# Single-row fetches of x on two queues replaced by POOL gathers in a graph layer

## The chip, the cores and the metric

The kernel runs on one core of a Trainium2 chip. The metric is the device time of one execution in microseconds; ten executions of the kernel before have a median of 1937.29 us (1935.77 to 1938.89). A profiled execution gives the trace from which everything below is read. Its time is the span from the first to the last instruction, with a little around it.

The names used for the engines are PE (TensorE), ACT (ScalarE), DVE (VectorE), POOL (GpSimd) and SP (SyncE). ACTq, SPq and POOLq are the instruction queues of these engines: there they issue DMAs, move registers and wait.

## What is computed

One message-passing layer over 12,500 nodes with 64 features and 200,000 edges sorted by target node, then a residual and a layer norm. In all of it `ssp(v)` is `softplus(v) - log 2`:

```
nodes       = x[[src, dst]].reshape(E, 128)                 # two rows of x per edge
gates       = (ssp(edge_attr @ We1 + be1) @ We2 + be2) * soft_cutoff(edge_weight)
h           = ssp(nodes @ Wn1 + bn1) @ Wn2 + bn2
message_sum = zeros.at[dst].add(h * gates)                  # sum of the messages by target node
new         = x + ssp(message_sum @ Ws1 + bs1) @ Ws2 + bs2
out         = layernorm(x + new)
```

The part that the change is about is `x[src]`: for each edge one row of 64 floats (256 bytes) of `x`, in DRAM, at an index known only at run time. The rows `x[dst]` are handled otherwise, since the targets are sorted.

## The kernel before, in words

**Groups and slots.** The edges are cut into NG = 391 groups of 512. A group has K = 4 slots of 128 edges, one edge per partition. A slot needs 128 rows of `x`, one per partition, in a tile of 128 x 128 floats: columns 0 to 63 take the row, columns 64 to 105 a one-hot of the edge's target inside a window of 42 nodes. The last slot of the last group is padding, so 1563 slots have to be filled.

**Two ways to fill a slot.** Most slots are filled by `gather` (L221): for each slot of group `g` one indirect DMA at L231, issued by POOL, reads 128 indices from `src_i` and fetches 128 rows into the tile `xg` of the group. `xg` has 19 buffers (`AHEAD` + `BEHIND`), so that POOL can run some 14 groups ahead. The other 47 slots, chosen by `slots_by_rows` (L105), are filled row by row: SP fills 21 of them (slot 3 of some groups) and ACT 26 (slot 2 of some groups). Each row is one ordinary DMA of 256 bytes, at L257 in `fetch`, whose source address is a register. `read_rows` (L245) loads eight such addresses at a time from the tile `rows_i` into registers. The destination is one of two tiles per queue, `xr`, with semaphores of its own (`landed`); `onehot` copies the slot's one-hot into it (L296), and the transpose of the slot (L304) waits for all of its 128 rows.

**One step.** The main loop (L632) does this for one `i` after another, the order of each engine written out by hand. SP issues the loads for group `i + 5` (`load`: the edge features at L278, and at L286 two windows of 42 rows of a table of target rows) and then seven rows of its fetch. POOL issues `gather(i + 14)`. PE transposes the four slots of group `i + 1` (`transposes`, L307, or L304 for a slot by rows). ACT copies the result to SBUF (`xcopy`, L314) and then issues three rows of its fetch. PE does the bias matmuls (L319, L354), the scatter of an older group's messages (L383: messages times one-hots), the two halves of layer 1 (L324, L330). ACT takes `exps` (L341), three rows, `logs` (L344), three rows: nine rows a step. PE does layer 2 of group `i` (L361, L366), DVE its cut and messages (L375, L379), the running sum by node (L400), `softplus` (L349) and the one-hots of group `i + 3` (L293).

From step 378 (`CLOSE`) on the scatter runs one group behind, not two, and step 378 does two scatters. When the sums of a block of 512 nodes are complete, parts of the node network and the layer norm of that block (`node_block`) are worked off among the following steps; L419 and L450 are its matmuls. The last two groups and the last block come after the loop.

**Before the loop** the table of `x @ Wn1[64:] + bn1` is computed for all nodes and written to DRAM (L591 to L595). While it is made, POOL already gathers the first 14 groups (L515). `rows_i` is loaded there (L509) and scaled to byte offsets (L600).

Of the kernel before, what the change touches and what calls it, by code (L numbers as in the profile page):

```python
# [42 lines left out]
F32 = mybir.dt.float32  # L43
BF16 = mybir.dt.bfloat16
I32 = mybir.dt.int32
U8 = mybir.dt.uint8
AF = mybir.ActivationFunctionType
OP = mybir.AluOpType
# [9 lines left out]
P = 128  # L58
D = 64
# [3 lines left out]
DW = D + W  # L63
PIECES = 3
NB = 512
K = 4
# [6 lines left out]


BLOCK_STEPS = ((2, 3, 4, 4, 6, 7, 8, 9, 10, 14), (2, 3, 3, 4, 5, 6, 7, 8, 9, 10), (1, 2, 1, 2, 3))
ROWS = (7, 9)
READ = 8
ROWS_FROM = -1
READY = (5, 7)
LANDED = 4  # L80
CUTOFF = 5.0
EPS = 1e-5
LN2 = 0.6931471805599453
# [18 lines left out]
    return steps  # L102


def slots_by_rows(NG):  # L105

    slots = []
    for queue in range(2):
        n = 0
        for g in range(READY[queue], NG - 2):  # L110
            if (g - READY[queue] - ROWS_FROM + 1) * ROWS[queue] >= (n + 1) * P:
                slots.append((queue, g, K - 1 - queue))
                n += 1
    return slots


def row_columns(NG):

    queues = [queue for queue, _, _ in slots_by_rows(NG)]
    return [-(-queues.count(queue) // READ) * READ for queue in range(2)]  # L120


@with_exitstack
def gnn_resnorm_kernel(ctx: ExitStack, tc: tile.TileContext, a: dict, out: bass.AP, E: int):
    nc = tc.nc
    x = a["x"]
    N = x.shape[0]
    NG = a["eT"].shape[1]
# [5 lines left out]
    assert NCH * P >= N - 1 + W and NR * P >= NH and 8 * D * N < 2**24  # L134
    REST = LOADS + 2

    rows_base = nc.sbuf_base + -nc.sbuf_base % 32
    nc.alloc_sbuf_tensor("rows", [P, 4 * P], F32)
    const = ctx.enter_context(tc.tile_pool(name="const", bufs=1))
    dram = ctx.enter_context(tc.tile_pool(name="dram", bufs=1, space=DRAM))  # L140
    loads = ctx.enter_context(tc.tile_pool(name="loads", bufs=LOADS + 2))
# [42 lines left out]
    rs3 = const.tile([PIECES, K, D], BF16, name="rs3")  # L184
    wns = const.tile([DW, REST, 2, 2 * D], F32, name="wns")

    xgs, xrs, eTs = {}, {}, {}
    made = {}

    def note(key, ins):  # L190
        made.setdefault(key, []).append(ins)
        return ins

    def behind(ins, *keys):

        for key in keys:
            for other in made.get(key, []):
                tc.add_manual_dep(ins.ins, other.ins.name,
                                  mybir.DependencyInfo(mybir.DependencyClass.Sync, mybir.DependencyReason.DATA),
                                  reason="one place of a step takes its waits")  # L200

    slots = slots_by_rows(NG)
    by_rows = {(g, k): n for n, (_, g, k) in enumerate(slots)}
    columns_of = row_columns(NG)
    rows_i = const.tile([P, sum(columns_of)], I32, name="rows_i")
    queues = (nc.sync, nc.scalar)
    firsts = (0, len([1 for queue, _, _ in slots if queue == 0]), len(slots))
    landed = [[tc.alloc_semaphore(f"rows{queue}_{i}") for i in range(LANDED)] for queue in range(2)]
    x_bytes = x.rearrange("(o n) d -> o (n d)", o=1).bitcast(U8)
    table_bytes = table.rearrange("(o n) d -> o (n d)", o=1).bitcast(U8)  # L210

    def arrived(g, k):
        n = by_rows[g, k]
        queue = slots[n][0]
        n -= firsts[queue]
        return landed[queue][n % LANDED], 16 * P * (n // LANDED + 1)

    def padding(g, k):
        return g * GE + k % 2 * HE + k // 2 * P >= E
# [1 line left out]
    def gather(g):  # L221

        xg = loads.tile([P, K, P], F32, name="xg", bufs=AHEAD + BEHIND)
        xgs[g] = xg
        for k in range(K):
            if (g, k) in by_rows:
                continue
            if padding(g, k):
                nc.vector.memset(xg[:, k, :D], 0.0)
                continue  # L230
            note(("gather", g), nc.gpsimd.indirect_dma_start(  # L231
                out=xg[:, k, :D], out_offset=None, in_=x,
                in_offset=bass.IndirectOffsetOnAxis(ap=src_i[:, g, k : k + 1], axis=0)))

    def rows_left(queue):
        return (firsts[queue + 1] - firsts[queue]) * P - fetched[queue]

    def read_rows(i, queue, count):

        count = min(count, rows_left(queue))  # L240
        while i >= ROWS_FROM and len(row_at[queue]) < count:
            q, p = divmod(fetched[queue] + len(row_at[queue]), READ * P)
            assert p % READ == 0
            at = queue * columns_of[0] + q * READ
            row_at[queue] += nc.values_load_multi_w_load_instructions(  # L245
                rows_i[p // READ : p // READ + 1, at : at + READ], engines=[queues[queue].engine], min_val=0,
                max_val=4 * D * (N - 1), skip_runtime_bounds_check_because="src holds rows of x")[1]

    def fetch(i, queue, count):

        for _ in range(min(count, rows_left(queue)) if i >= ROWS_FROM else 0):
            n, r = divmod(fetched[queue], P)
            n += firsts[queue]
            _, g, k = slots[n]
            if r == 0:
                row_tiles[n, "in"], xrs[g, k] = row_tile(queue, n), row_tile(queue, n)
            ins = queues[queue].dma_start(row_tiles[n, "in"][r : r + 1, :D].bitcast(U8),  # L257
                                          x_bytes[:, bass.ds(row_at[queue].pop(0), 4 * D)])
            tc.no_tile_sem_insts.add(ins.ins.name)
            ins.then_inc(arrived(g, k)[0], 16)  # L260
            if r == 0:
                behind(ins, ("rows read", n - 2))
            fetched[queue] += 1

    row_at, row_tiles, fetched = [[], []], {}, [0, 0]

    def row_tile(queue, n):
        return nc.alloc_sbuf_tensor_at(f"xr{queue}_{n % 2}", [P, P], F32,
                                       offset=rows_base + (2 * queue + n % 2) * 4 * P).ap()

    bases = {}

# [18 lines left out]

    def onehot(g):
        last = nc.vector.tensor_tensor(xgs[g][:, :, D:DW], iota, rel[:, g, :].to_broadcast([P, K, W]), OP.is_equal)  # L293
        for k in range(K):
            if (g, k) in by_rows:
                last = nc.vector.tensor_copy(xrs[g, k][:, D:DW], xgs[g][:, k, D:DW])  # L296
                behind(last, ("rows read", by_rows[g, k] - 2))
        note(("onehot", g), last)

    def transposes(g, *needs):  # L300
        tx = tx_tile()[:DW].rearrange("f (k e) -> f k e", k=K)
        for k in range(K):
            if (g, k) in by_rows:
                ins = nc.tensor.transpose(tx[:, k, :], xrs[g, k][:, :DW], ident)  # L304
                note(("rows read", by_rows[g, k]), ins.wait_op(*arrived(g, k), "sem-ge"))
            else:
                ins = nc.tensor.transpose(tx[:, k, :], xgs[g][:, k, :DW], ident)  # L307
            if k == 0:
                behind(ins, *needs)
        xTs[g] = tx  # L310
# [179 lines left out]
    with tc.manual_schedule():  # L490
# [4 lines left out]
        with tc.tile_pool(name="prep", bufs=1) as prep:  # L495
# [10 lines left out]

            for i in range(3):
                load_x(i)
            nc.sync.dma_start(rows_i, a["rows"])  # L509
            dist = cut.rearrange("p g k -> p (g k)")  # L510
            nc.sync.dma_start(dist, a["dist_l"])
            dst_i = rel.bitcast(I32)
# [73 lines left out]
            for i in range(PARTS):  # L586
# [10 lines left out]
                if i == 1:  # L597
                    nc.vector.tensor_copy(base_i[:1], base_b[:1])
                    nc.vector.tensor_scalar(base_i[32:33], base_b[32:33], float(8 * D), None, OP.mult)
                    nc.vector.tensor_scalar(rows_i, rows_i, float(4 * D), None, OP.mult)  # L600
                    for k in range(2):
                        nc.vector.tensor_copy(be3[:, k, :], rows[:, 0, :])
                    for k in range(K):
                        nc.vector.tensor_copy(row3[:, :, k, :], rows[:, 1:3, :])
                        nc.vector.tensor_copy(rs3[:, k, :], rows[:, 3, :])
# [9 lines left out]
        with tc.tile_pool(name="finish", bufs=1) as finish:  # L615
# [16 lines left out]
            for i in range(-1, last - 1):  # L632
                now = parts.pop(i, [])
                early = [part for part in now if part.tensor]
                at(load, i + LOADS)
                read_rows(i, 0, ROWS[0])
                fetch(i, 0, ROWS[0])
                if i >= 0:
                    at(gather, i + AHEAD)
                transposes(i + 1, ("load", i + 1), ("gather", i + 1), ("onehot", i + 1))  # L640
                xcopy(i + 1)
                read_rows(i, 1, ROWS[1])
                fetch(i, 1, ROWS[1] - 6)
                layer1_bias(i + 1)
                at(layer2_bias, i)
                for n, g in enumerate(behind_by(i)):
# [1 line left out]
                layer1_edge(i + 1)  # L648
                layer1_node(i + 1)
                exps(i + 1)  # L650
                fetch(i, 1, 3)
                logs(i + 1)
                fetch(i, 1, 3)
                for g in behind_by(i):
                    window(g)
                at(layer2, i)
# [143 lines left out]
def layouts(inputs):  # L800
# [12 lines left out]
    def padded(v, n, fill):  # L813
        return np.concatenate([v, np.full((n - v.shape[0],) + v.shape[1:], fill, v.dtype)])
# [4 lines left out]

    out = {"x": np.ascontiguousarray(x)}  # L820
    out["src_l"] = lanes(src, 0)
    rows = []
    for queue, columns in enumerate(row_columns(NG)):
        chosen = [out["src_l"].reshape(P, NG, K)[:, g, k] for q, g, k in slots_by_rows(NG) if q == queue]
        v = padded(np.concatenate(chosen), P * columns, 0).reshape(-1, P, READ)
        rows.append(v.transpose(1, 0, 2).reshape(P, columns))
    out["rows"] = np.ascontiguousarray(np.concatenate(rows, axis=1))
    out["dst_l"] = lanes(dst, dst[-1])
    out["dist_l"] = lanes(dist, 1e6)
    out["dst_h"] = np.ascontiguousarray(padded(dst, NR * P * HE, dst[-1]).reshape(NR, P, HE).transpose(1, 0, 2))  # L830
# [42 lines left out]
```

## Time and profile before

| | |
|---|---|
| median of ten runs | 1937.29 us |
| the profiled execution, its time | 1937.95 us |
| the profiled execution, its span | 1936.2 us |
| mean granted clock of PE | 0.972 |
| first row fetch on ACT's queue, on SP's queue (start) | 77.9 us, 81.0 us |
| last row fetch on ACT's queue, on SP's queue (start) | 1813.4 us, 1871.7 us |
| first and last gather on POOL (start) | 3.3 us, 1905.5 us |
| DMA packets, data moved | 150911, 143.53 MB |

How to read it. A group of instructions is given by its line, engine and operation, then `out<-in` by the names of the tiles, the count, the busy time in all and the mean of one in ns, and behind the bar the idle time of the engine just before these instructions with what ended most of it. "issue" is idle time in which the engine waited for nothing that the profile shows. A row of waits is: engine, what it was about to do, what it waited for, us in total, number of times, the longest. A timeline row is: start, duration, engine, line, operation, tiles, shapes, count, and in brackets the idle time before it. Issuing a DMA, moving a register or waiting is not counted as busy, except the gathers on POOL, which POOL works on itself. The spans on POOL are rough.

### The profile page before, as it was taken

Reading aid. Unit: us, or ns where it says so; the run is one execution under the profiler, and the core shown is the slowest. Engines: PE = TensorE matmul, PEld = TensorE weight load, DVE = VectorE, ACT = ScalarE, POOL = GpSimd, SP = SyncE. Lnnn points to the kernel's source line nnn. Section 1 sums busy time; section 2 is a strip of 40 time slices with the busy share of each in tenths; the row PEclk is TensorE's granted clock in tenths of the full one; section 3 lists DMA queues with packets and bytes.
Section 4 is the critical chain, followed back from the end, with each engine's and each line's share of the span. In section 5 each row is a group of like instructions: output and inputs, shape, how many; then the busy total and the mean of one; then the engine's idle time right before and its main releaser. Section 6 shows DMA issues by size and latency. Waiting matters only on the chain.

```text
span 1936.2 us, 47845 instructions
## 1 busy us (share of the span) xinstructions
PE 1789.9 (92%) x11373; PEld 1467.1 (76%) x11373; DVE 1052.9 (54%) x2767; ACT 964.0 (50%) x1318; POOL 1441.0 (74%) x1520
## 2 busy tenths in 40 slices
PE   4899999999999998999999999999999999999997
PEld 4787777877887777777777777777777777777775
DVE  4355555555465554555555555555555555555555
ACT  1255554545455554545555555454454554555543
POOL 7777777777777777777777777777777777777772
PEclk9999999999899999999999999999999999999998
DMA  8422222322222323332322322233223333323321
GB/s 247 132 66 69 65 65 66 71 66 65 68 70 69 68 66 70 71 70 66 71 67 68 76 67 71 68 70 75 68 70 70 71 70 70 73 68 76 74 67 24
DMA packets 150911, 143.53 MB, mean 74 GB/s; under 512 B 51887, under 2 KB 98395, under 8 KB 150626
## 3 DMA queue, kind: packets, MB, share of 16 engines
q1 hardware_dynamic: 94090, 88.26, 16.0%
q0 software_dynamic: 48512, 49.77, 14.1%
q10 hardware_dynamic: 8024, 2.37, 0.6%
q8 instruction: 97, 1.59, 0.3%
q14 instruction: 188, 1.54, 0.3%
HBM read 130.59 MB, written 9.63 MB: 72 GB/s over the span
## 4 chain that ended last, share of the span: by engine, by line
PE 54%; ACTq 13%; issue 8%; SPq 7%; DMA 7%; ACT 6%; DVE 3%; POOL 1%; DVEq 0%; POOLq 0%
PE z L330 12%; ACTq L257 11%; PE gh L366 9%; PE z L383 8%; PE tx L307 6%; PE z L324 6%; PE gh L361 5%; SPq L257 3%; DMA xg<-in_x,src_i 3%; PE gh L354 3%; ACT xT L314 3%; PE z L319 3%; DMA wns<-table 2%; ACTq L245 2%; ACT u L341 2%
## 5 line engine op out<-in xcount | busy, mean ns | idle before, releaser
L231 POOL DMA_INDIRECT xg<-in_x,src_i x1516 | 1440.7, 950 | 465.3 <-issue 358.3
L341 ACT ACTIVATE u<-z 128x768 f32<-128x768 f32 x392 | 317.3, 809 | 698.2 <-PE z L330 660.5
L400 DVE TENSOR_TENSOR sums<-sums,z 64x42 f32 x778 | 152.9, 197 | 771.9 <-ACT u L341 735.2
L330 PE MATMUL z<-xT,wns 106*128 106x256 f32 x1564 | 433.7, 402 | 8.7 <-ACT xT L314 7.9
L344 ACT ACTIVATE u<-u,one 128x768 f32<-128x768 f32 x392 | 366.1, 934 | 70.1 <-ACT u L341 65.5
L366 PE MATMUL gh<-consts,s 128*128 128x64 f32 x3128 | 398.0, 271 | 0.0
L366 PEld LDWEIGHTS gh<-consts,s 128*128 128x128 f32 x3128 | 387.7, 195 | 0.1
L349 DVE SCALAR_TENSOR_TENSOR s<-u,z 128x768 f32<-128x768 f32 x392 | 369.6, 943 | 12.3 <-ACT u L344 10.2
L330 PEld LDWEIGHTS z<-xT,wns 106*128 106x128 f32 x1564 | 303.1, 199 | 81.2 <-ACT xT L314 36.1
L307 PE MATMUL tx<-consts,xg 128*106 128x128 f32 x1517 | 236.7, 276 | 87.8 <-DMA wns<-table 25.5
L383 PEld LDWEIGHTS z<-xg,msg 128*128 128x128 f32 x1556 | 206.2, 193 | 125.5 <-issue 121.2
L314 ACT COPY xT<-tx 106x512 f32<-106x512 f32 x391 | 228.1, 583 | 126.5 <-PE tx L307 106.0
L383 PE MATMUL z<-xg,msg 128*128 128x84 f32 x1556 | 266.8, 294 | 0.9 <-DVE msg L379 0.2
L361 PEld LDWEIGHTS gh<-consts,s 128*128 128x128 f32 x1564 | 247.5, 199 | 25.5 <-DVE s L349 2.0
L324 PE MATMUL z<-eT,consts 128*128 128x256 f32 x782 | 258.4, 413 | 0.0
L307 PEld LDWEIGHTS tx<-consts,xg 128*106 128x106 f32 x1517 | 168.8, 140 | 105.2 <-PE gh L366 52.9
L361 PE MATMUL gh<-consts,s 128*128 128x128 f32 x1564 | 246.9, 281 | 1.7 <-DVE s L349 1.7
L375 DVE TENSOR_TENSOR h<-gh,cut 128x256 f32<-128x256 f32 x391 | 166.1, 425 | 32.8 <-PE gh L366 18.7
L379 DVE TENSOR_TENSOR msg<-gh,h 128x256 f32<-128x256 f32 x391 | 165.9, 424 | 13.4
L354 PE MATMUL gh<-row,ones 3*128 3x512 bf16 x391 | 147.4, 377 | 0.0
L293 DVE TENSOR_TENSOR xg<-consts,rel 128x168 f32<-128x168 f32 x391 | 128.6, 329 | 0.0
L324 PEld LDWEIGHTS z<-eT,consts 128*128 128x128 f32 x782 | 122.7, 198 | 1.5 <-issue 1.5
(93 smaller groups left out, 586.7 us busy)
## 6 DMA issues: line engine op xcount, KB each, us to landing
xr<-in_x ACTq DMA_DIRECT2D x3328, 0.2 KB
eT<-in_eT SPq DMA_DIRECT2D x195, 256.0 KB
xr<-in_x SPq DMA_DIRECT2D x2688, 0.2 KB
xg<-in_x,src_i POOLq DMA_INDIRECT x1516
wns<-table SPq DMA_DIRECT2D x782, 21.0 KB
table<-tb SPq DMA_DIRECT2D x14, 448.0 KB
sums<-in_xT SPq DMA_DIRECT2D x7, 455.0 KB
y<-in_x SPq DMA_DIRECT2D x24, 128.0 KB
```

The costliest lines, as they stand in the source:

```text
L231: note(("gather", g), nc.gpsimd.indirect_dma_start(out=xg[:, k, :D], out_offset=None, in_=x, in_offset=bass.IndirectOffsetOnAxis(ap=src_i[ ...
L257: ins = queues[queue].dma_start(row_tiles[n, "in"][r : r + 1, :D].bitcast(U8), x_bytes[:, bass.ds(row_at[queue].pop(0), 4 * D)])
L307: ins = nc.tensor.transpose(tx[:, k, :], xgs[g][:, k, :DW], ident)
L314: note(("xcopy", g), nc.scalar.copy(xT, xTs[g]))
L324: nc.tensor.matmul(zs[g][:, 0, :HE], we1.rearrange("a h d -> a (h d)"), eTs[g], start=False, stop=True, skip_group_check=True)
L330: nc.tensor.matmul(zn, wns[:, g % REST, h, :], xTs[g][:, h], start=True, stop=True, skip_group_check=True)
L341: nc.scalar.activation(us[g][:, part], z_of(g)[:, part], AF.Exp)
L344: nc.scalar.activation(us[g][:, part], us[g][:, part], AF.Ln, bias=one)
L349: nc.vector.scalar_tensor_tensor(ss[g].rearrange("p i t e -> p (i t e)")[:, part], us[g][:, part], BIG, z_of(g)[:, part], OP.min, OP.max)
L361: nc.tensor.matmul(v[:, 0, t], ss[g][:, 0, t, :], we2, start=False, stop=False, skip_group_check=True)
L366: nc.tensor.matmul(ghs[g][:, 1, 2 * t + h, :], ss[g][:, 1 + h, t, :], wn2, start=False, stop=h == 1 and t == 1, skip_group_check=True)
L383: ins = nc.tensor.matmul(sc, msgs[g][:, 2 * t : 2 * t + 2, :].rearrange("p h f -> p (h f)"), xgs[g][:, 2 * t : 2 * t + 2, D:DW], start=t = ...
```

## The change

All 1563 slots are filled by POOL's gathers. `fetch`, `read_rows`, the list of slots, the tiles `xr` and `rows_i`, their semaphores, the copy of the one-hot into `xr` and the second form of the transpose are removed. Nothing else moves: the order of the loop, the tiles, the number of buffers and the preparation stay.

```diff
-ROWS = (7, 9)
-READ = 8
-ROWS_FROM = -1
-READY = (5, 7)
-LANDED = 4
...
-def slots_by_rows(NG):
...
-def row_columns(NG):
...
-    rows_base = nc.sbuf_base + -nc.sbuf_base % 32
-    nc.alloc_sbuf_tensor("rows", [P, 4 * P], F32)
...
         for k in range(K):
-            if (g, k) in by_rows:
-                continue
             if padding(g, k):
                 nc.vector.memset(xg[:, k, :D], 0.0)
                 continue
             note(("gather", g), nc.gpsimd.indirect_dma_start(
                 out=xg[:, k, :D], out_offset=None, in_=x,
                 in_offset=bass.IndirectOffsetOnAxis(ap=src_i[:, g, k : k + 1], axis=0)))
-
-    def rows_left(queue):
...
-    def read_rows(i, queue, count):
...
-    def fetch(i, queue, count):
...
     def onehot(g):
         last = nc.vector.tensor_tensor(xgs[g][:, :, D:DW], iota, rel[:, g, :].to_broadcast([P, K, W]), OP.is_equal)
-        for k in range(K):
-            if (g, k) in by_rows:
-                last = nc.vector.tensor_copy(xrs[g, k][:, D:DW], xgs[g][:, k, D:DW])
-                behind(last, ("rows read", by_rows[g, k] - 2))
         note(("onehot", g), last)
...
         for k in range(K):
-            if (g, k) in by_rows:
-                ins = nc.tensor.transpose(tx[:, k, :], xrs[g, k][:, :DW], ident)
-                note(("rows read", by_rows[g, k]), ins.wait_op(*arrived(g, k), "sem-ge"))
-            else:
-                ins = nc.tensor.transpose(tx[:, k, :], xgs[g][:, k, :DW], ident)
+            ins = nc.tensor.transpose(tx[:, k, :], xgs[g][:, k, :DW], ident)
...
-            nc.sync.dma_start(rows_i, a["rows"])
...
-                    nc.vector.tensor_scalar(rows_i, rows_i, float(4 * D), None, OP.mult)
...
                 at(load, i + LOADS)
-                read_rows(i, 0, ROWS[0])
-                fetch(i, 0, ROWS[0])
                 if i >= 0:
                     at(gather, i + AHEAD)
                 transposes(i + 1, ("load", i + 1), ("gather", i + 1), ("onehot", i + 1))
                 xcopy(i + 1)
-                read_rows(i, 1, ROWS[1])
-                fetch(i, 1, ROWS[1] - 6)
                 layer1_bias(i + 1)
...
                 exps(i + 1)
-                fetch(i, 1, 3)
                 logs(i + 1)
-                fetch(i, 1, 3)
```

More of the change, by code (lines that the diff above doesn't have):

```diff
@@ L102, in block_steps @@
     return steps
-def slots_by_rows(NG):
[L107 to L114, printed above, removed]
-def row_columns(NG):
-    queues = [queue for queue, _, _ in slots_by_rows(NG)]
-    return [-(-queues.count(queue) // READ) * READ for queue in range(2)]
 @with_exitstack
@@ L185, in gnn_resnorm_kernel @@
     wns = const.tile([DW, REST, 2, 2 * D], F32, name="wns")
-    xgs, xrs, eTs = {}, {}, {}
+    xgs, eTs = {}, {}
     made = {}
@@ L200, in behind @@
                                   reason="one place of a step takes its waits")
[L202 to L209, printed above, removed]
-    table_bytes = table.rearrange("(o n) d -> o (n d)", o=1).bitcast(U8)
[L212 to L216, printed above, removed]
+    table_bytes = table.rearrange("(o n) d -> o (n d)", o=1).bitcast(U8)
     def padding(g, k):
@@ L233, in gather @@
                 in_offset=bass.IndirectOffsetOnAxis(ap=src_i[:, g, k : k + 1], axis=0)))
-    def rows_left(queue):
-        return (firsts[queue + 1] - firsts[queue]) * P - fetched[queue]
-    def read_rows(i, queue, count):
[L240 to L247, printed above, removed]
-    def fetch(i, queue, count):
[L251 to L269, printed above, removed]
     bases = {}
@@ L821, in layouts @@
     out["src_l"] = lanes(src, 0)
[L822 to L827, printed above, removed]
     out["dst_l"] = lanes(dst, dst[-1])
```

## The prediction, written before the changed kernel ran

> **What bounds the kernel now.** I read the page's busy shares first. TensorE, at 92%, looks like the bound, and POOL, at 74%, like an engine with a quarter of the span to spare. Shares cannot settle it, so the next views are POOL's own waits, with its idle time by what ended it, the number of times and the longest, and the page's row of the gathers:
>
> ```profile
> PE 1789.9 (92%) x11373; PEld 1467.1 (76%) x11373; DVE 1052.9 (54%) x2767; ACT 964.0 (50%) x1318; POOL 1441.0 (74%) x1520
> ...
> POOL 7777777777777777777777777777777777777772
> ...
> L231 POOL DMA_INDIRECT xg<-in_x,src_i x1516 | 1440.7, 950 | 465.3 <-issue 358.3
> ```
>
> ```profile
> POOL xg L231 <- issue: 358.3, 1174, 0.3
> POOL xg L231 <- DMA xg<-in_x,src_i: 27.8, 91, 0.3
> POOL xg L231 <- PE z L330: 17.4, 57, 0.3
> ```
>
> The last column is what matters: no idle stretch of POOL before a gather is longer than 0.3 us, whoever is named as its end, except 2.9 us for the first index load. The other engines named in that view only happened to finish then. The timeline of POOL shows the rhythm: start, duration, and the same 0.30 to 0.31 us before every gather.
>
> ```profile
> 14.40 0.95 POOL L231 DMA_INDIRECT xg<-in_x,src_i  x1 [0.31 <-issue]
> 15.65 0.94 POOL L231 DMA_INDIRECT xg<-in_x,src_i  x1 [0.30 <-issue]
> ...
> 1903.04 0.94 POOL L231 DMA_INDIRECT xg<-in_x,src_i  x1 [0.30 <-issue]
> 1904.29 0.95 POOL L231 DMA_INDIRECT xg<-in_x,src_i  x1 [0.30 <-issue]
> 1905.55 0.94 POOL L231 DMA_INDIRECT xg<-in_x,src_i  x1 [0.30 <-issue]
> ```
>
> So POOL issues gathers from 3.35 to 1905.55 us without a pause; one takes 1.25 us from start to start. The "74%" is a saturated queue. Whether TensorE waits for it is read by counting: I laid the start of each group's last gather (in program order, row slots left out) beside the same group's L319, which follows its transposes at once. TensorE is behind that gather by 69 us at group 0 (7.2 against 76.3), 35 at group 100 (497.8, 533.1), 9 at group 200 (983.5, 992.8) and 3.7 at group 230 (1129.0, 1132.7). From there to group 378 the distance stays at 3.2 to 6.6 us, mostly 3.2 to 4: landing and transposes, no store left. At group 380 it is 8.7, at group 390 it is 6.1. So the lead that POOL builds while the table is made is used up by 1130 us, and then POOL sets the pace. TensorE's own step is shorter. These are starts of one step's transposes after the other's, near the end:
>
> ```profile
> 1883.62 0.60 PE L307 MATMUL tx<-consts,xg 128*106 128x128 f32 x4
> ...
> 1887.90 0.60 PE L307 MATMUL tx<-consts,xg 128*106 128x128 f32 x4
> ...
> 1892.17 0.60 PE L307 MATMUL tx<-consts,xg 128*106 128x128 f32 x4
> ...
> 1911.14 0.60 PE L307 MATMUL tx<-consts,xg 128*106 128x128 f32 x4
> ```
>
> A step without a node part takes 4.27 us (1887.90 to 1892.17); one with such a part is longer, and groups 380 to 390 average 4.5. Four gathers take POOL 4 x 1.253 = 5.01 us. The last line is group 390; from its 1911.14 to the end of the span are 25.1 us.
>
> **What the change adds.** 2688 + 3328 rows are 6016, and 6016 / 128 = 47 slots. All 47 become gathers at L231: 1516 + 47 = 1563. The durations are on the page: 0.94 us busy and 0.30 us of issue. The mean pitch from gather 56 (77.29 us) to the last (1905.55) is 1828.26 / 1459 = 1.253 us, stalls included. 47 x 1.253 = **+58.9 us** on the last gather. Bounds: 1.24, the shortest distances, give 58.3; 1.2556, the mean over all 1516 with the stalls of the first 75 us, gives 59.0. No wait is added, and what is queued behind each new gather on POOL is the next gather.
>
> The Trainium skill, DMA: Bandwidth & Descriptors, section "Issuing engines are not separate DMA queues", speaks against this: all issuers end on the same DMA engines, and several issuers only save sequencer time, which is usually small beside the transfer. By that rule moving the slots would cost about nothing and the sum would stay near 0. Here the issuer's 1.25 us is the thing that runs out, while the page's DMA row stands at two to three tenths.
>
> **What it removes, and what hides that.** ScalarE's queue loses 3328 row DMAs at 0.223 us with their moves of 0.029, and 416 register loads of median 0.742, some 1150 us of issue; SP loses 2688 at 0.257 and 336 at 0.804, some 960 us:
>
> ```profile
> L257 ACTq MOVE xr<-in_x x3328: 29/29/41, 77.9 to 1813.4; - x196
> L257 ACTq DMA_DIRECT2D xr<-in_x x3328: 222/223/593, 78.0 to 1813.5; - x196
> ```
>
> These issues hold `xcopy`, `exps` and `logs` behind them, and the chain of waits gives ScalarE's queue 13% and SP's 7% of the span. I take nothing for their removal: it quickens TensorE's step, and that hides under POOL's 5.01 us. The cover is 5.01 - 4.27 = 0.74 us a plain step; if POOL did not pace, all the issue time on the chain could come back at most, 20% of 1936 = 387 us, and at least nothing. The window loads (L286) that were late behind SP's fetches, 25.5 us of TensorE's wait, go the same way: next late is `xg`. VectorE loses 47 copies (L296) of 0.186 us, 8.7 us on an engine 54% busy: nothing. The load and scaling of `rows_i` in the preparation lie before TensorE's first step, with 69 us of lead behind it: nothing. The 47 transposes only change their source (273 ns against 276).
>
> The Trainium skill, SBUF — State Buffer, section "Who interferes with whom", would credit the removed copies to POOL: VectorE and GpSimd share a port pair that a copy in a two-port mode can hold. By that rule up to 8.7 us could come back. The trace barely agrees: of the 54 gathers after 100 us that took over 0.97 us, 4 overlap one of the 44 copies that the timeline lists singly.
>
> The 54 long gathers together exceed the norm by 5.9 us. If their cause were the fetches in any way, the gain would be 5.9 at most; if unrelated, 0. I take 0, since long ones are rare before 600 us too, where fetches run.
>
> **The end.** Behind the last gather come its landing and 25.1 us of last steps and last node block, untouched. What can shrink is TensorE's distance: 6.1 us at group 390 against 3.3 for a group that is taken when it lands. It jumps at group 379 to 380, where two scatters fall in one step and matmuls run at half pace for a step (L330 1.91 us, not 1.03), and then shrinks. From group 380 to 390 TensorE took 45.2 us for its steps and POOL 47.7; with the one row slot of this stretch (at 1898) back on POOL, POOL takes 49.0. With the same jump of 8.7 the distance at the end is 8.7 + 45.2 - 49.0 = 4.9, which is 1.2 less than now. Ends: 3.3 (2.8 less) and 8.7 (2.6 more).
>
> **Sum.** +58.9 - 1.2 = +57.7; I take 57.5. Span 1936.2 + 57.5 = 1993.7. That execution took 1937.95, 1.75 around its span; the median of the runs is 1937.29, 0.7 below it. So 1937.3 + 57.5 = **1994.8 us**.
>
> **Rivals.**
> A, faster: the 0.30 us between gathers is itself caused by the thousands of other DMAs, so POOL quickens when they go, and the freed queues pay. For: 20% of the chain is those two queues. Against: the gathers from 4.7 to 75 us, before the first row fetch at 77.9, show the same 0.30. It decides once the mean pitch is below (1905.55 - 3.35) / 1562 = 1.218 us. At POOL's 0.95 alone TensorE would run free at about 4.5 us: 76.3 + 390 x 4.5 + 24.5 = 1856.
> B, no change: the 14 groups of lead swallow the 47 gathers. For: 69 us of lead exceed 58.9. Against: the lead is spent by group 230. Price 0: 1937.
> C, much slower: a starved TensorE runs its steps at half pace. Such a step (1326.06 to 1331.83) takes 5.77 us, more than 5.01. If every step behind the catching-up were so, from about group 130 (52 us of distance at group 20, shrinking by 0.36 to 0.71 a group): 260 x 0.76 = 198 more, 2192. Against: a slow step leaves TensorE late, the next finds its data there and runs in 4.1 to 4.3; the present distances stay at 3.2 to 6.6.
>
> **How the numbers follow.** The forecast holds 0.92, A 0.015, B 0.015, C or another larger loss 0.05. Range: least 1937.3 + 58.3 - 2.8 - 2.8 (half of the long gathers' 5.9, rounded) = 1990; most 1937.3 + 59.0 + 2.6 = 1998.9, so 1999. About 0.2% (4 us) is what a measurement here can tell from no change. Faster 0.015, the same 0.015, slower 0.97.
>
> **What would show it.** POOL with 1563 gathers at the same 0.94 and 0.30, the last starting near 1964.5; distance near 3.3 us already from some group between 95 and 165, that is from 480 to 830 us; TensorE waiting for `xg` for more than 100 us in all where it now waits 18.0; ScalarE and SP queues without L257 and L245, and off the chain. Wrong if the pitch leaves 1.24 to 1.26, if POOL shows waits over 0.3 us, or if the tail behind the last transposes leaves 24 to 27 us.

## The result and the profile after

The changed kernel takes 1994.58 us, the median of 8 runs (1992.98 to 1996.48), against 1937.29 before: a ratio of 1.0294, 95% interval 1.0285 to 1.0303. It is 57.3 us slower. The profiled execution has a span of 1994.0 us. One thing has to be known for what follows: the experiments ran on three chips, of which one ran the kernel before in 1936.23 us and two in 2672.56 and 2638.19 us, at granted clocks of 0.81 to 0.84, so each run is told by its ratio to the kernel before on its own chip.

The page of the kernel after, busy shares, POOL's and DMA's row of slices, the chain and two groups (the line numbers have moved: L190 is the gather, L222 the transpose, L234 the first matmul behind it):

```profile
PE 1789.4 (90%) x11373; PEld 1480.7 (74%) x11373; DVE 1040.7 (52%) x2719; ACT 953.6 (48%) x1318; POOL 1487.3 (75%) x1567
...
POOL 7777777777777777777777777777777777777773
...
DMA  8422222222222232223222222222222232222221
...
PE 78%; DMA 9%; DVE 4%; issue 4%; POOL 2%; SPq 1%; ACT 1%; DVEq 0%; POOLq 0%; ACTq 0%
...
L190 POOL DMA_INDIRECT xg<-in_x,src_i x1563 | 1487.1, 951 | 479.6 <-issue 341.7
...
L222 PE MATMUL tx<-consts,xg 128*106 128x128 f32 x1564 | 240.6, 277 | 159.4 <-DVE msg L294 62.4
```

The shares have hardly moved: POOL from 74 to 75%, TensorE from 92 to 90%. Nothing in that first line says that 57 us were lost, or where. The gathers' row does: 1563 instead of 1516, 951 ns each instead of 950. The chain shows the two queues gone (ScalarE's 13% and SP's 7% are 0 and 1%), and the kernel is slower all the same.

POOL's waits and its timeline in the kernel after:

```profile
POOL xg L190 <- issue: 341.7, 1121, 0.3
POOL xg L190 <- DMA xg<-in_x,src_i: 58.4, 190, 0.6
POOL xg L190 <- PE z L245: 40.0, 131, 0.3
```

```profile
1963.70 0.94 POOL L190 DMA_INDIRECT xg<-in_x,src_i  x1 [0.30 <-PE z L245]
1964.94 0.94 POOL L190 DMA_INDIRECT xg<-in_x,src_i  x1 [0.30 <-issue]
1966.19 0.94 POOL L190 DMA_INDIRECT xg<-in_x,src_i  x1 [0.30 <-issue]
```

It is the same rhythm with 6016 other DMAs gone: 0.94 and 0.30. Leaving out the first index load (2.9 us), two waits alone are longer than that, 0.57 and 0.53 us, both while the table is still being made:

```profile
17.81 0.94 POOL L190 DMA_INDIRECT xg<-in_x,src_i  x1 [0.57 <-DMA xg<-in_x,src_i]
19.27 0.99 POOL L190 DMA_INDIRECT xg<-in_x,src_i  x1 [0.53 <-DMA xg<-in_x,src_i]
```

The last gather of group 70 with that group's transposes, and the transposes of the last group, on TensorE:

```profile
363.98 0.94 POOL L190 DMA_INDIRECT xg<-in_x,src_i  x1 [0.30 <-DVE msg L294]
...
367.00 0.62 PE L222 MATMUL tx<-consts,xg 128*106 128x128 f32 x4
...
1969.42 0.60 PE L222 MATMUL tx<-consts,xg 128*106 128x128 f32 x4
```

The span can be added up from three places: the start of the last gather, the distance from there to the first matmul behind the last transposes (L319, now L234), and the rest. The kernels before and after, and two experiments that are told below:

| us | before | after | no row fetches, 47 slots unfilled | SyncE's rows only |
|---|---|---|---|---|
| gathers on POOL | 1516 | 1563 | 1516 | 1542 |
| mean pitch from gather 56 on | 1.2531 | 1.2538 | 1.2538 | 1.2537 |
| start of the last gather | 1905.55 | 1966.19 | 1907.36 | 1939.18 |
| distance at group 390 | 6.1 | 3.8 | 5.2 | 4.8 |
| rest to the end of the span | 24.5 | 24.1 | 24.2 | 24.6 |
| span | 1936.2 | 1994.0 | 1936.7 | 1968.6 |
| TensorE's step, groups 10 to 50 | 4.34 | 4.09 | 4.09 | 4.38 |

From before to after the last gather moves by 60.6: 47 x 1.2538 = 58.9 for the gathers, 0.75 because gather 56 already starts later (78.04 against 77.29), and 1.0 because the pitch is 0.7 ns longer over 1459 gathers. The distance gives back 2.4, the rest 0.4. 60.6 - 2.4 - 0.4 = 57.8, the difference of the spans (1994.0 - 1936.2).

### The profile page after: what moved, and what is told of

Read it like the earlier page. It is cut to its first block, busy times and chain, and to the rows that moved or that the text cites. A ratio compares the mean times of both kernels' runs of the same rounds, so it can differ in the third digit from the quotient of the medians.

```text
span 1994.0 us, 35107 instructions
## 1 busy us (share of the span) xinstructions
PE 1789.4 (90%) x11373; PEld 1480.7 (74%) x11373; DVE 1040.7 (52%) x2719; ACT 953.6 (48%) x1318; POOL 1487.3 (75%) x1567
## 4 chain that ended last, share of the span: by engine, by line
PE 78%; DMA 9%; DVE 4%; issue 4%; POOL 2%; SPq 1%; ACT 1%; DVEq 0%; POOLq 0%; ACTq 0%
PE z L245 16%; PE gh L281 13%; PE z L298 11%; PE tx L222 10%; PE z L239 9%; PE gh L276 7%; DMA xg<-in_x,src_i 5%; PE gh L269 4%; PE z L234 4%; DVE h L290 2%; DMA wns<-table 2%; POOL xg L190 2%; PE z L505 2%; DVE msg L294 1%; PE tx L334 1%
## 5 line engine op out<-in xcount | busy, mean ns | idle before, releaser
L190 POOL DMA_INDIRECT xg<-in_x,src_i x1563 | 1487.1, 951 | 479.6 <-issue 341.7
L245 PE MATMUL z<-xT,wns 106*128 106x256 f32 x1564 | 427.2, 397 | 0.6 <-ACT xT L229 0.6
L281 PE MATMUL gh<-consts,s 128*128 128x64 f32 x3128 | 397.7, 271 | 0.0
L281 PEld LDWEIGHTS gh<-consts,s 128*128 128x128 f32 x3128 | 387.7, 195 | 0.1
L222 PE MATMUL tx<-consts,xg 128*106 128x128 f32 x1564 | 240.6, 277 | 159.4 <-DVE msg L294 62.4
L245 PEld LDWEIGHTS z<-xT,wns 106*128 106x128 f32 x1564 | 311.3, 199 | 50.5 <-ACT xT L229 3.4
L222 PEld LDWEIGHTS tx<-consts,xg 128*106 128x106 f32 x1564 | 167.8, 136 | 187.6 <-issue 82.6
```

Source lines behind the costliest of these rows:

```text
L190: note(("gather", g), nc.gpsimd.indirect_dma_start(out=xg[:, k, :D], out_offset=None, in_=x, in_offset=bass.IndirectOffsetOnAxis(ap=src_i[ ...
L245: nc.tensor.matmul(zn, wns[:, g % REST, h, :], xTs[g][:, h], start=True, stop=True, skip_group_check=True)
L281: nc.tensor.matmul(ghs[g][:, 1, 2 * t + h, :], ss[g][:, 1 + h, t, :], wn2, start=False, stop=h == 1 and t == 1, skip_group_check=True)
```

## The experiments

The theory is that POOL's queue sets the end at 1.2538 us a gather once its lead is spent, and that the row fetches neither cost nor gained anything at the end. Its rival is that the freed queues matter on their own, so that the 57 us are a larger loss less a gain. Four runs were made on the chip where the kernel before is at 1936.23 us, and the main readings are from these; eight were made on the other two chips.

**Neither fetched nor gathered.** Against the kernel after, `skip` holding the 47 slots that rows had filled before:

```diff
         for k in range(K):
+            if (g, k) in skip:
+                continue
             if padding(g, k):
```

> The same 47 slots are filled by nobody: neither row fetches nor gathers; the slots keep the rows of an older group. POOL issues 1516 gathers as in the kernel before, SyncE and ScalarE fetch nothing. Theory (POOL's queue sets the end at 1.2537 us a gather, the row fetches cost nothing at the end): 1994.6 - 47 x 1.2537 = 1935.7 us, 1934 to 1938, the time of the kernel before. Rival (the freed queues pay on their own, and POOL's loss was larger than the difference that was measured): below 1925 us.

Measured: 1937.84 us (1937.11 to 1938.51), ratio to the kernel before 1.0006, interval 0.9996 to 1.0015. The rival needed less than 1925. So with the same number of gathers as before, and without a single one of the 6016 row DMAs, their 752 register loads and 47 copies, the time is that of the kernel before. The span and the gathers' row on the page of this run, then its last gather and the transposes of the last group:

```profile
span 1936.7 us, 34994 instructions
...
L206 POOL DMA_INDIRECT xg<-in_x,src_i x1516 | 1443.2, 952 | 464.6 <-issue 327.3
```

```profile
1907.36 0.94 POOL L206 DMA_INDIRECT xg<-in_x,src_i  x1 [0.30 <-issue]
...
1907.95 0.60 PE L238 MATMUL tx<-consts,xg 128*106 128x128 f32 x4
```

12,851 instructions fewer than the 47,845 of before, and 0.5 us of span. This separates the two halves of the change: the removal is worth nothing at the end that this measurement can tell (0.15% at most, some 3 us), and the 47 gathers are the loss.

**SyncE's rows alone.** Against the kernel before:

```diff
-    for queue in range(2):
+    for queue in (0,):
         n = 0
...
```

> SyncE fetches its 21 slots by rows again, ScalarE none; POOL gathers 1542 slots. Theory: 1994.6 - 21 x 1.2537 = 1968.3 us, last gather near 1939.9 us. Rival (ScalarE's freed queue gave part of the loss back): below 1960 us. It also tells which queue had lengthened TensorE's step in groups 10 to 50 (4.34 us before, 4.09 after): ScalarE's if it stays near 4.09 here, SyncE's if it is near 4.34.

Measured: 1971.43 us (1970.44 to 1972.52), ratio 1.0178, interval 1.0161 to 1.0195. The last gather starts at 1939.18 us, where 1939.9 was expected; the time is 3.1 above the forecast and 11 above what the rival needed. Against the kernel after the last gather starts 27.0 us earlier, and the distance and the last steps are 1.6 longer, which makes the spans differ by 25.4; the medians differ by 23.2, where 26.3 were forecast. ScalarE's queue held 13% of the old chain, and taking all its fetches away brought no time beyond what the gathers explain.

```profile
1939.18 0.94 POOL L231 DMA_INDIRECT xg<-in_x,src_i  x1 [0.30 <-issue]
```

The run also shows that SyncE's fetches are enough to lengthen TensorE's step while POOL still has its lead: with SyncE fetching alone the step is 4.38 us, without any fetch 4.09. The same stretch of time in three kernels, in the table of windows (length, then busy us and instruction counts of TensorE's matmuls, its weight loads, VectorE, ScalarE and POOL, the clock, DMA); first before, then SyncE alone, then after:

```profile
125.00:280.00 155.00, 150.99 (x1011) 121.49 (x1010) 85.55 (x220) 83.98 (x108) 117.17 (x124) 1.00 0.29 67
```

```profile
125.00:280.00 155.00, 149.22 (x993) 124.88 (x993) 82.96 (x214) 81.31 (x107) 117.29 (x124) 0.98 0.28 66
```

```profile
125.00:280.00 155.00, 155.00 (x1063) 130.16 (x1062) 88.85 (x229) 86.33 (x114) 117.47 (x124) 1.00 0.30 71
```

Without fetches TensorE does not stop once in 155 us and gets 5% more matmuls done (1063 against 1011). POOL's column is the same in all three, 124 gathers. That is the gain of the change in one row; it comes to nothing at the end, since TensorE only reaches POOL sooner.

**POOL relieved.** Against the kernel after:

```diff
         for k in range(K):
+            if k == 3 and AHEAD + BEHIND <= g < NG - 2:
+                continue
             if padding(g, k):
```

> Slot 3 of groups 19 to 388 is filled by nobody: POOL issues 1193 gathers instead of 1563, the last near 1498 us if it never waits. Theory (TensorE's own step is 4.1 to 4.5 us with the node parts, 5.01 only because of POOL): 79 + 390 x 4.35 + 25 = 1800 us, 1742 to 1860. Rival (TensorE's step is near 4.85 to 5 us for reasons of its own and POOL's pace is a coincidence): 1936 us or more.

Measured: 1759.22 us (2 runs, 1758.04 and 1760.4), ratio 0.9081, interval 0.9063 to 0.9099. That is inside the theory's range and far below the rival's 1936. The page and POOL's waits:

```profile
PE 1706.9 (97%) x11373; PEld 1427.0 (81%) x11373; DVE 1040.0 (59%) x2719; ACT 940.9 (54%) x1318; POOL 1175.4 (67%) x1197
...
PE 96%; DMA 2%; DVE 1%; ACT 1%; issue 0%; SPq 0%; DVEq 0%; ACTq 0%
```

```profile
POOL xg L192 <- PE z L300: 154.8, 287, 1.7
```

This is how POOL looks when it is not the bound: it waits up to 1.7 us for the scatter matmul (L300 here) that frees a buffer, 287 times, its mean pitch is 1.395 us, and the distance of TensorE behind it stays at 60 to 70 us from group 50 on instead of falling to 3.5. The expected start of the last gather, 1498 us, was wrong for the reason that its own sentence left open: POOL did wait, and the last one started at 1662.86. TensorE's step is 4.16 us over groups 50 to 150. As an estimate, 1994.58 - 1759.22 = 235 us is what POOL's pace costs the kernel after.

**The gathers doubled.** Against the kernel after, each of the 47 slots is gathered twice into the same place:

```diff
-            note(("gather", g), nc.gpsimd.indirect_dma_start(
...
+            for _ in range(2 if (g, k) in twice_of else 1):
+                note(("gather", g), nc.gpsimd.indirect_dma_start(
...
```

> The 47 slots that the change moved to POOL are gathered twice, each time into the same place: 1610 gathers, nothing else changed against the kernel after. Theory: 1994.6 + 47 x 1.2537 = 2053.5 us. Rival (part of the 57 us came with the removal of the row fetches, not with the gathers): clearly less than 59 us more, for instance 20 to 40.

Measured: 2133.18 us (2 runs), 138.6 more than the kernel after, where 58.9 were expected. Both theory and rival miss. POOL's waits and one pair of twins in its timeline:

```profile
POOL xg L205 <- DMA xg<-in_x,src_i: 119.7, 218, 2.9
```

```profile
124.38 0.94 POOL L205 DMA_INDIRECT xg<-in_x,src_i  x1 [0.30 <-issue]
127.04 0.94 POOL L205 DMA_INDIRECT xg<-in_x,src_i  x1 [1.72 <-DVE xg L231]
```

The second gather writes where the first writes, and waits until the first has landed: by the trace's records of landings, each second one starts 0.26 us (six times 0.76) after its twin's last landing. The start of this one is 2.66 us after its twin's; the 47 such pitches run from 2.65 to 3.79 and exceed 1.25 us by 81.7 together. 58.9 + 81.7 = 140.6, about the 138.6 found. So the edit added a wait that was not meant, and the run says nothing against the price of a gather. What it gives is the time from a gather's start to its landing, 2.4 us at least. That is most of the floor under the distance: in the kernel after the median landing is 2.5 us, a transpose that waited for it starts 0.35 to 0.46 later, and the transposes take some 0.55, together 3.4 to 3.5 (the distance there is 3.4 at least).

The same with the extra gathers going to spare tiles that nobody reads was run on the chip at 2638.19 us:

```diff
+            if (g, k) in twice_of:
+                nc.gpsimd.indirect_dma_start(
+                    out=loads.tile([P, D], F32, name="spare", bufs=4), out_offset=None, in_=x,
...
```

> As the kernel after, with 47 extra gathers of the slots that the change moved, this time into spare tiles that nobody reads, so that no extra gather waits for the landing of its twin. 1610 gathers. Theory (each gather costs POOL's pitch of 1.2538 us and nothing else): 1994.6 + 58.9 = 2053.5 us. Rival (a gather's price grows with their number, through transfers or landings): near the 2133 us of the run with the twins in one place, or anything over 2065.

Measured: 2704.98 us against 2638.19 for the kernel before there, ratio 1.0257, interval 1.0157 to 1.0358. Both expected times were meant for a chip at 1937; this decides nothing between them.

**The other runs on those chips.** On the chip at 2672.56 us three of the edits above were run (SyncE's rows alone, 47 slots unfilled, 370 slots unfilled) and ScalarE's rows alone (`for queue in (1,):`), which was also run on the chip at 2638.19.

> SyncE fetches its 21 slots by rows again, ScalarE none; POOL gathers 1542 slots. Theory (POOL's queue sets the end at 1.2537 us a gather, and the row fetches themselves cost or gain nothing at the end): 1994.6 - 21 x 1.2537 = 1968.3 us, last gather near 1966.2 - 26.3 = 1939.9 us. Rival (freeing ScalarE's queue, 13% of the old chain, gave part of the loss back, so POOL's price per slot is above 1.25 and ScalarE's fetches cost time of their own): below 1960 us, with less than its share left for the run with ScalarE alone. It also tells which of the two queues had lengthened TensorE's step in groups 10 to 50 (4.34 us before, 4.09 after): ScalarE's if it stays near 4.09 here.

> ScalarE fetches its 26 slots by rows again, SyncE none; POOL gathers 1537 slots. Theory: 1994.6 - 26 x 1.2537 = 1962.0 us, last gather near 1933.6 us. Rival (ScalarE's fetches cost time of their own): above 1970 us. TensorE's step in groups 10 to 50 near 4.34 us if ScalarE's issues are what lengthened it, near 4.09 if SyncE's.

> The same 47 slots are filled by nobody: neither row fetches nor gathers, the slots keep the rows of an older group. POOL issues 1516 gathers as in the kernel before, SyncE and ScalarE fetch nothing. Theory: 1994.6 - 47 x 1.2537 = 1935.7 us, 1934 to 1938, the time of the kernel before, since the row fetches cost nothing at the end. Rival (the freed queues pay on their own and the loss of POOL was larger than the difference): below 1925 us.

> Slot 3 of groups 19 to 388 is filled by nobody (it keeps an older group's rows): POOL issues 1193 gathers instead of 1563, the last near 3.4 + 1192 x 1.2537 = 1498 us if it never waits, and TensorE is released from it. Theory (TensorE's own step is 4.1 to 4.5 us with the node parts, 5.01 only because of POOL): 79 + 390 x 4.35 + 25 = 1800 us, 1742 to 1860. Rival (TensorE's step is near 4.85 to 5 us for reasons of its own and POOL's pace is a coincidence): 1936 us or more.

> ScalarE fetches its 26 slots by rows again, SyncE none; POOL gathers 1537 slots. Theory: 1994.6 - 26 x 1.2538 = 1962.0 us, last gather near 1934 us, and TensorE's step in groups 10 to 50 stays at 4.09 us, since with SyncE alone fetching it was 4.38. Rival (ScalarE's issues, 13% of the old chain, cost time of their own): above 1970 us and a step over 4.2.

| run | us | before there | ratio, 95% interval |
|---|---|---|---|
| SyncE's rows alone | 2620.12 | 2672.56 | 0.975 (0.967 to 0.983) |
| ScalarE's rows alone | 2633.14 | 2672.56 | 0.983 (0.975 to 0.990) |
| 47 slots unfilled | 2625.32 | 2672.56 | 0.981 (0.975 to 0.987) |
| 370 slots unfilled (one run) | 2135.7 | 2672.56 | |
| ScalarE's rows alone, other chip | 2583.47 | 2638.19 | 0.980 (0.970 to 0.989) |

None of the expected times can be compared with these. What the table shows is that the theory has a condition. Here 26 or 21 gathers more than before went with a time 2% shorter, not 1 to 2% longer. The waits of three engines in the run with 47 slots unfilled:

```profile
POOL xg L206 <- PE z L314: 353.0, 113, 62.5
DVE h L306 <- remote: 234.9, 79, 5.9
ACT xT L245 <- remote: 198.4, 78, 5.6
POOL xg L206 <- remote: 167.8, 80, 2.7
```

POOL waits for the scatter that frees its buffers, once for 62.5 us and otherwise up to 6 us at a time, and TensorE stays 87 to 105 us behind it (groups 230 to 378), not 3 to 7: POOL is not the bound there. The same kernel between 1000 and 1500 us, on the chip at 1936.23 us and on this one:

```profile
1000.00:1500.00 500.00, 459.52 (x2964) 378.43 (x2962) 271.22 (x716) 250.28 (x351) 378.42 (x400) 0.98 0.28 67
```

```profile
1000.00:1500.00 500.00, 410.28 (x2249) 332.44 (x2248) 201.99 (x530) 190.17 (x260) 293.56 (x310) 0.82 0.22 51
```

TensorE does 2964 matmuls in this stretch on the one chip and 2249 on the other. On the second, ScalarE and VectorE also stand still together, 74 times and for up to 5.9 us, until a release that the view calls "remote": it can put it to nothing in the profile of this core. At one such stall, which ended at 1205.6 us, TensorE had been idle since 1200.5. What holds them was not found. One run with 370 slots unfilled took 2135.7 us there, 490 less than with 47 unfilled, though POOL was not the bound in it either (TensorE is 68 to 85 us behind); why is open as well. The kernel after itself was not run there, so whether the change costs anything on such a chip is open.

**More rows instead of fewer.** If each row slot saves 1.25 us, more of them should beat the kernel before.

```diff
-ROWS = (7, 9)
+ROWS = (9, 9)
```

The second run has `(9, 12)`.

> The other way: the kernel before with nine rows a step on SyncE instead of seven, so 27 + 26 = 53 slots by rows and 1510 gathers. Theory (POOL still sets the end): 6 x 1.2538 = 7.5 us less than before, 1929.8 us. Rival (SyncE's queue is full at nine rows, its window loads come late and TensorE's step exceeds POOL's): no gain or slower than before.

> Nine rows a step on SyncE and twelve on ScalarE: 27 + 35 = 62 slots by rows, 1501 gathers. Theory: 15 x 1.2538 = 18.8 us less than before, 1918.5 us, as long as the queues hold out: ScalarE's would issue 12 x 0.252 + 1.5 x 0.742 = 4.1 us a step, POOL's pace is (1563 - 62) / 391 x 1.2538 = 4.81 us a step. Rival (the queues become the bound): above 1930 us, with POOL waiting for buffers.

Measured on the chip at 2638.19 us: 2753.98 and 2755.83, ratios 1.046 (1.038 to 1.054) and 1.043 (1.035 to 1.051). On that chip more rows are a loss of 4%. On a chip at 1937 us they were not run, so that more rows than in the kernel before would pay is not shown.

## Why the prediction was right, and where its steps were not

**POOL is saturated at 74%.** Right, and shown twice: with 1516 gathers and no fetches the time is the old one, and with 1193 gathers POOL waits and TensorE sets the end.

**+58.9 for the gathers.** Right in size: 47 x 1.2538. The last gather moved by 60.6, 1.7 more than the term and 1.6 above its upper bound of 59.0: 0.75 were lost in the first 78 us and 1.0 in a pitch 0.7 ns longer. What causes these two was not found.

**Nothing for the long gathers.** Right. Counted alike in both traces (over 0.97 us, after 100 us), there are 55 before and 55 after, 6.0 and 7.7 us above the usual 0.944 (the prediction counted 54 and 5.9): they did not go with the fetches, so the half of 5.9 us that the lower end of the range allows for was not there to be had.

**Nothing for the freed queues.** Right at the end (ratio 1.0006 without them), and right that the gain hides under POOL's 5.01 us. Before that end it is larger than was reckoned with. The step "shrinking by 0.36 to 0.71 a group" put the point where TensorE has used up the lead at group 95 to 165; it came at group 70, near 367 us. The step had taken TensorE's pace from groups in which SyncE was fetching, 4.3 to 4.65 us. Without fetches it is 4.09, so the distance shrinks by 0.92 a group.

**The distance at the end.** Right in sign, small by half: 2.4 less, not 1.2. The assumed term was "the same jump of 8.7". After the step with two scatters the distance in the kernel after is 5.6 at group 380, and 3.8 at group 390.

**Twenty-five microseconds of last steps.** 25.0 before and 24.6 after, from the start of the last transposes to the end, where no change was forecast; the layer 2 matmuls of the last group (L366, now L281) took 1.97 us for eight before and 1.35 after.

The forecast stands on one product. The single terms miss by 1.7, 1.2 and 0.4 us; that they cancel to 0.2 us in the time (1994.58 against 1994.8) is luck.

**What would show it.** The pitch (1.2538), the last gather (1966.19 against 1964.5), the last steps and the idle queues are as said. "Wrong if POOL shows waits over 0.3 us" did occur, with the waits of 0.57 and 0.53 us at 17.8 and 19.3 us; they cost 0.5 us beyond the usual gap, and there is none later, so the sign was set too tight and the mechanism stands. The distance fell at group 70 and not between 95 and 165, as told above. The last sign, "TensorE waiting for `xg` for more than 100 us", seems to fail in the view of TensorE's waits after:

```profile
PE tx L222 <- DVE msg L294: 62.4, 58, 1.3
PE tx L222 <- DMA wns<-table: 24.3, 20, 6.5
PE tx L222 <- DVE h L290: 24.1, 39, 1.0
PE tx L222 <- DMA xg<-in_x,src_i: 18.3, 15, 1.7
```

The row named `xg` is 18.3, about as before. All idle time ahead of the transposes grew from 87.8 (L307) to 159.4 us, and more than half of it is put down to VectorE's messages and cuts, on which by the order of the program no transpose depends. The trace also records when each gather lands, and that settles it: among the 345 groups of the kernel after whose last gather has a full record, 175 have transposes that waited over 0.1 us, and 171 of these, 130 us in all, start 0.2 to 0.5 us behind the last landing of the group's last gather. In the kernel before it is 55 of 92 among 318 groups, and 34 us. So the sign came true, and the view's row hid it.

**The rivals.** A (POOL quickens when the other DMAs go) falls with the pitch: 1.2538 without them. B (the lead swallows the gathers) falls with the distance, 3.6 at group 70 already. C (half-paced steps all along) falls too: the distances from group 70 on stay at 3.4 to 7.0 us.

## What to carry to other kernels

A queue whose instructions follow one another at a fixed interval, with idle gaps that are all of one length, is full whatever its busy share; count its instructions and multiply by the interval. Before giving such a queue more work, compare how far its consumer is behind it over the run: where that distance has fallen to little more than the landing time, as here on the chips at 1937 us, each added instruction is paid in full, and work taken from other engines is worth nothing at the end. To split a change that removes one thing and adds another, run it with the added part left out: here that one kernel separated a zero from 57 us.

## What the runs showed that was not expected

With two gathers into the same place the second starts 2.65 to 3.79 us after the first instead of 1.25: POOL's queue stands still until the first has landed, and everything behind it with it.

A row of waits named after other engines can be a wait for a gather: 18.3 us stand in the row of `xg`, and by the landings it is 130.

SyncE's 21 slots of row fetches alone lengthen TensorE's step from 4.09 to 4.38 us, as much as both queues together (4.34). Beside SyncE's, ScalarE's 26 slots add nothing that shows, with a larger share of the chain; ScalarE's alone were run only on the slower chips.

The same instructions can have another bound on another chip: with 47 slots unfilled the kernel is level with the one before where that takes 1936 us (ratio 1.0006) and 1.9% faster where it takes 2673.
